# Masked float32r comparisons for the last eight source tiles in the second layer of a four-layer graph network

## The chip, the cores and the metric

The kernel runs on one core of a Trainium2 chip. The metric is the device time of one execution in microseconds (us); the kernel before takes 3552.45 us (median of three runs). The core's engines work side by side, each through its own queue in order: TensorE (PE; its weight loads are shown as PEld), VectorE (DVE), ScalarE (ACT), GpSimd (POOL), and SyncE (SP), which here only issues DMAs.

## The reference

A graph of 3327 nodes with 512 features and a 0/1 adjacency matrix goes through four layers; each adds its result to x. The first three are graph attention layers with 8, 4 and 8 heads, the fourth is a mean over neighbours with dense projections. The change lies in the second (it is called layer 1 in the code, which counts from 0):

```python
def _L1_gnn_ref(H, A, W, a_l, a_r):
    n = H.shape[0]
    mask = A + jnp.eye(n, dtype=A.dtype) > 0
    Wh = (H @ W).reshape(n, N_HEADS, D_K)             # 4 heads of 128
    sl = jnp.einsum('nhd,hd->nh', Wh, a_l)
    sr = jnp.einsum('nhd,hd->nh', Wh, a_r)
    e = jax.nn.leaky_relu(sl[:, :, None] + sr.T[None, :, :], negative_slope=0.2)
    e = jnp.where(mask[:, None, :], e, -jnp.inf)
    alpha = jnp.nan_to_num(jax.nn.softmax(e, axis=2), nan=0.0)
    out = jnp.einsum('nhm,mhd->nhd', alpha, Wh).reshape(n, 512)
    return jax.nn.elu(out)
# each layer:
h = jnp.maximum(_layernorm(x, axis=-1), 0.0)
x = x + _L1_gnn_ref(h, adj, L1_gnn_W, L1_gnn_a_l, L1_gnn_a_r)
```

## The kernel before

**The idea.** The exponential of leaky_relu(s1 + s2) is a product of a factor of the destination and a factor of the source, with one pair of factors where s1 + s2 > 0 and another where it is not. So the softmax numerator and denominator are two plain matrix products per head: a 0/2 matrix "adjacent and s1 > -s2" times the source rows with the first factor (sign a = 0), and "adjacent and s1 <= -s2" times the rows with the second (a = 1). No exponential is taken per edge; what has to be made per head are the two 0/2 matrices, transposed, with sources on the partitions.

**Tiling.** The 3327 nodes are 26 tiles of 128. Destinations are worked on in seven chunks of four tiles (`PER`; the last has two). Sources are in five groups `JG`: 6, 6, 6, 4 and 4 tiles. For each chunk c and head h (28 pairs in this layer) `attention` loads the chunk's scores s1 onto all partitions (`s1b`, line 682, two buffers), and for each sign and group the source rows (`ab`, line 714, seven buffers, ten loads per pair).

**The matrices before.** `matrices` makes, per group, a tile `tht` in fp8 (ten buffers) with one comparison per source tile and 512 destinations, on ScalarE (line 670) or, for the source tiles listed in `GP_ON_DVE`, on VectorE (line 667). In this layer the list has tiles 18 to 25, the two groups of four. A bitwise AND with the group's mask on VectorE (line 674) leaves the matrix of the first sign. The masks, fp8 zeros and twos, lie in `m` tiles (six buffers, line 271), reloaded for each chunk. When all matmuls of the first sign have read a tile, a bitwise XOR with the mask (line 794) turns it into the second sign's in place.

**The products.** `KIND = "bssvv"` says how each group is multiplied. Group 0 ("b") uses the fp8 tile as it is, against source rows in three bf16 pieces, 387 columns (line 762). The other four use float32r, 258 columns (line 759), and their matrices must be copied from fp8 to float32r: `real` does so per sign and per pass, groups 1 and 2 ("s") on ScalarE into `ts` (three buffers, 6 tiles x 256 destinations), groups 3 and 4 ("v") on VectorE into `tv` (two buffers, 4 tiles x 256 destinations), both at line 639.

A pass is two destination tiles (`ks`) against all 26 sources: per sign two passes, so four per pair, each 12 matmuls of 387 columns and 40 of 258. After a pass VectorE sums the three (or two) pieces of each accumulator into `R` (line 780). After the fourth it scales, adds and divides (lines 802 to 809). Accumulators have four buffers.

**Work in between.** After each pass `hooks.run` moves the tiles of the last finished chunk on by a stage: residual and elu (lines 866 to 870), layer norm (345 to 357), transposes (138, 142), projection for the next layer (413) and its factors (433 to 469 and 387 to 397). The order of instructions on each engine is not written out: a scheduler places them, with a few ordering hints (`after`), so an edit here can move others.

Of the kernel before, what the change touches and what calls it, by code (L numbers as in the profile page):

```python
# [29 lines left out]
FP8 = mybir.dt.float8e4  # L30
F32R = mybir.dt.float32r
AF = mybir.ActivationFunctionType
ALU = mybir.AluOpType
# [4 lines left out]
P = 128  # L38
# [4 lines left out]
S2_MAX = 30.0  # L43
S_CLIP = 40.0

GP_ON_DVE = [(5, 12, 19), tuple(range(18, 26)), (4, 9, 14, 19, 24)]


KIND = "bssvv"


@with_exitstack
def tile_gnn(ctx: ExitStack, tc: tile.TileContext, x, adj, W0, a01, W1, al, ar, W2, a2,
             Ws, bs, Wn, bn, Wc, bc, out):
    nc = tc.nc
# [8 lines left out]
    PER = 4  # L64
    chunks = [(t, min(PER, NT - t)) for t in range(0, NT, PER)]
    where = {t0 + k: (c, k) for c, (t0, n) in enumerate(chunks) for k in range(n)}
    JG = [(0, 6), (6, 6), (12, 6), (18, 4), (22, 4)]
    JM = max(n for _, n in JG)
# [45 lines left out]
    for l in range(3):  # L114
        H, DA, AO, HW = dims(l)
# [515 lines left out]
            while self.tiles or self.flying:  # L631
                self.run(1, 0, 0)

    def real(a, g, ks, th):

        nj = JG[g][1]
        k0, k1 = ks[0], ks[-1] + 1
        t = mp.tile([P, 2, nj, P], F32R, name="ts" if KIND[g] == "s" else "tv", bufs=3 if KIND[g] == "s" else 2)
        (nc.scalar.copy if KIND[g] == "s" else nc.vector.tensor_copy)(t[:, :k1 - k0, :nj], th[a][g][:, k0:k1])  # L639
        return t  # L640

    ahead = {}
# [42 lines left out]
    def attention(L, hooks, open_next, close):  # L685

        l = L.l
        H, DA, AO, HW = dims(l)
        DK = DA - 1
        masks = mask_tiles(0, l == 1) if l else masks0  # L690
        for c, (t0, nt) in enumerate(chunks):
            last = c + 1 == len(chunks)
            A = [mp.tile([P, D], F32, name="A", bufs=A_BUFS[l]) for _ in range(nt)]
            hook = 0
            for h in range(H):
# [8 lines left out]
                s1v = early.pop("s1") if "s1" in early else score_rows(l, t0, nt, h)  # L704
                ab = []
                for a in range(2 if l == 1 else 1):
                    row = []
                    for g, (_, nj) in enumerate(JG):
                        if l == 1:
                            tl = mp.tile([P, JM * 2 * DA], F32R, name="ab", bufs=7)  # L710
                            two = KIND[g] != "b"
                            w = 2 * DA if two else AO
                            v = (tl if two else tl.bitcast(BF16))[:, :nj * w].rearrange("p (j w) -> p j w", j=nj)
                            ld = nc.sync.dma_start(v.bitcast(F32) if two else v, abd[l][g][h, a])
                        else:
                            if g in ahead:
                                v = ahead.pop(g)
                            else:
                                v = pieces_tile(L, mp if l else bp, g)
                                ld = nc.sync.dma_start(v, abd[l][g][h])  # L720
                        row.append(v)
                    ab.append(row)
# [3 lines left out]
                th, flip = [[], []], []  # L726
                for g in range(len(JG)):
                    if g in early:
                        pv, gv = early.pop(g)
                    else:  # L730

                        pt = mp.tile([P, PER * JM * P], FP8, name="tht", bufs=10 if l == 1 else 7)
                        gt = pt if l == 1 else mp.tile([P, PER * JM * P], FP8, name="gt", bufs=7)
                        pv, gv, words, steps = matrices(L, nt, h, g, s1v, masks[g], pt, gt)
                        for step in steps:
                            step()
                        if l == 1:
                            flip.append(words)
                    th[0].append(pv)
                    th[1].append(gv)  # L740
                R = mp.tile([P, PER, 2, DA], F32, name="R", bufs=1)
                deg = l == 0 and h == 0
                for a in range(2 if l == 1 else 1):
                    passes = [(range(k0, min(nt, k0 + 2)), range(NT)) for k0 in range(0, nt, 2)]
                    if c == 0 and h == 0 and a == 0:
                        cut = JG[-1][0]
                        passes = [(ks, range(0, cut)) for ks, _ in passes] + [(ks, range(cut, NT)) for ks, _ in passes]
                    acc = {}
                    for ks, js in passes:
                        thr = {}  # L750
                        for j in js:
                            g, jj = jwhere[j]
                            if l == 1 and KIND[g] != "b" and g not in thr:
                                thr[g] = real(a, g, ks, th)
                            for k in ks:
                                if j == 0:
                                    acc[k] = accs.tile([P, 512], F32, name="acc")
                                if g in thr:
                                    mm = nc.tensor.matmul(acc[k][:, :2 * DA], thr[g][:, k - ks[0], jj, :], ab[a][g][:, jj, :],  # L759
                                                     start=(j == 0), stop=(j == NT - 1), skip_group_check=True)  # L760
                                elif l == 1:
                                    mm = nc.tensor.matmul(acc[k][:, :3 * DA], th[a][g][:, k, jj, :], ab[a][g][:, jj, :3 * DA],  # L762
                                                     start=(j == 0), stop=(j == NT - 1), skip_group_check=True)
                                else:
                                    o = 1 if deg else 0
                                    nc.tensor.matmul(acc[k][:, :3 * DA + o], th[0][g][:, k, jj, :],  # L766
                                                     ab[0][g][:, jj, :3 * DA + o], start=(j == 0), stop=False,
                                                     skip_group_check=True)
                                    mm = nc.tensor.matmul(acc[k][:, AO:AO + 3 * DA + o], th[1][g][:, k, jj, :],  # L769
                                                     ab[0][g][:, jj, AO:AO + 3 * DA + o], start=False, stop=(j == NT - 1),  # L770
                                                     skip_group_check=True)
                            if j == JG[3][0]:
                                late = mm.ins.name
                        if l == 2 and last and h == H - 1:
                            load_y2(yp, 0, late)
                        if js[-1] != NT - 1:
                            continue
                        for k in ks:
                            if l == 1:
                                nc.vector.tensor_reduce(R[:, k, a, :], acc[k][:, :3 * DA].rearrange("p (s d) -> p d s", s=3),  # L780
                                                        AX.X, ALU.add)
                            else:
                                v = acc[k][:, :2 * AO].rearrange("p (a w) -> p a w", a=2)[:, :, :3 * DA]
                                nc.vector.tensor_reduce(R[:, k], v.rearrange("p a (s d) -> p a d s", s=3), AX.X, ALU.add)  # L784
                            if deg:
                                n = pn(t0 + k)
                                nc.vector.tensor_reduce(deg2[:n, t0 + k:t0 + k + 1],
                                                        acc[k][:n, 3 * DA:AO + 3 * DA + 1:AO], AX.X, ALU.add)
                        gone.append(mm.ins.name)
                        hooks.run(1 if last else 3, hook, 2 if hook % 2 and c == 0 or hook % 3 == 0 and c else 1, 2 if last else 1)  # L790
                        hook += 1
                    if a == 0:
                        for pu, mu in flip:
                            nc.vector.tensor_tensor(pu, pu, mu, ALU.bitwise_xor)
                        if h == H - 1 and not last:
                            pending = loops
# [21 lines left out]
            masks = nmasks  # L818
# [79 lines left out]
    with tc.tile_pool(name="first", bufs=1) as fp:  # L898
# [19 lines left out]
        L = open_layer(0)  # L918
# [10 lines left out]
        while hooks.tiles or hooks.flying:  # L929
# [4 lines left out]
            for g in range(3):  # L934
                if n == (8, 15, 21)[g]:
# [6 lines left out]
                    s = PER * JM * P  # L942
                    pv, gv, _, steps = matrices(L, PER, 0, g, early["s1"], masks0[g], b[:, :s], b[:, s:2 * s])
                    hooks.small += steps
                    early[g] = pv, gv
        while hooks.small:
            hooks.small.pop(0)()
    A, R = [("A", D, F32, n) for n in A_BUFS], ("R", PER * 2 * 129, F32, 1)
    ab, gt, tht = ("ab", JM * 400, BF16, 7), ("gt", PER * JM * P, FP8, 7), ("tht", PER * JM * P, FP8, 7)
    tags = [[A[0], ("R", PER * 2 * 65, F32, 1), tht, ("tr", JM * P, BF16, 5), ("abx", 4 * 400, BF16, 4), gt],  # L950
            [A[1], ("ab", JM * 258, F32R, 7), R, ("ts", 2 * JM * P, F32R, 3), ("tv", 2 * 4 * P, F32R, 2), tht[:3] + (10,)],
            [A[2], ab, ("R", PER * 2 * 65, F32, 1), tht, gt]]
    hooks.masks = in_steps([mask_steps(ip, t, g) for t, g in order[20:]])
    for l in range(3):
# [3 lines left out]
        mp = att.enter_context(tc.tile_pool(name=f"att{l}", bufs=1, reuse_waits="tile"))  # L958
# [526 lines left out]
```

## Time and profile before

| what | value |
|---|---|
| runs | 3546.64, 3552.45 and 3554.89 us |
| span of the profiled execution, first to last instruction | 3551.1 us |
| granted TensorE clock, mean of the span | 0.990 |
| TensorE busy, whole span | 3442.3 us (97%) |
| VectorE busy | 2624.3 us (74%) |
| ScalarE busy | 2507.0 us (71%) |
| GpSimd busy | 618.8 us (17%) |
| first and last matmul on `ts` (line 759) | 1248.3 and 2070.1 us |
| VectorE waiting for TensorE ahead of line 639, second layer | 55.1 us in 27 waits, longest 5.5 |
| ScalarE waiting for TensorE ahead of line 639 | 52.5 us in 39 waits, longest 3.9 |
| VectorE waiting for ScalarE ahead of line 794 | 19.4 us in 13 waits, longest 4.5 |

A profile line of an instruction group reads: line of the code, engine, operation, output<-input with shapes and types, count | busy us, mean ns of one | idle time of the engine just before them, and what ended most of it. "128x1024" is 128 partitions by 1024 elements. A line of the timeline begins with the start and the length of a merged run of equal instructions, in us; in brackets stands the idle time before it and what ended it. A line of waits reads: who waited, for whom, us in total, times, longest. Matmuls overlap: one of 283 ns starts every 120 ns, so only their start times tell the rate.

### The profile page before, as it was taken

The numbers are of one execution on the slowest core, as the hardware profiler recorded it, in microseconds if no ns is written. First come the engines' busy times: TensorE is split into PE (matmuls) and PEld (weight loads), VectorE is DVE, ScalarE is ACT, GpSimd is POOL, SyncE is SP. The second block draws the span as 40 slices with busy tenths as digits, with TensorE's granted clock in tenths as the row PEclk, the third lists the DMA queues.
The fourth block names the chain that finished last, engine by engine and source line by source line (L and its number), as shares of the span: only waits on it lengthen the run. The fifth ranks groups of instructions, "written<-read, shape, count | busy, mean of one in ns | idle before, by whom it ended". The sixth has DMA issues, their size and how long they took to land. (4 is left out here: it accounts for less than half of the span.)

```text
span 3551.1 us, 77646 instructions
## 1 busy us (share of the span) xinstructions
PE 3442.3 (97%) x30751; PEld 3107.2 (88%) x30751; DVE 2624.3 (74%) x5227; ACT 2507.0 (71%) x4113; POOL 618.8 (17%) x858
## 2 busy tenths in 40 slices
PE   7899999999999999999999989999999999999998
PEld 6789999999999888888888869989898989876887
DVE  7788888888887699888888868867676768672121
ACT  5777787878787789888888677767666757572111
POOL 6611222112111202222223320101010101020000
PEclk9999999999999999999999999999999999999999
DMA  7699999999857787777777875555545555576331
GB/s 207 223 282 251 233 263 238 268 260 250 256 203 247 246 285 276 279 269 273 269 273 254 332 268 190 191 175 189 183 166 181 185 172 188 168 271 257 105 107 54
DMA packets 398120, 797.72 MB, mean 225 GB/s; under 512 B 112970, under 2 KB 221845, under 8 KB 397105
## 3 DMA queue, kind: packets, MB, share of 16 engines
q1 hardware_dynamic: 363890, 723.14, 63.4%
q0 software_dynamic: 28128, 62.42, 7.6%
q10 hardware_dynamic: 5726, 7.08, 0.6%
q8 instruction: 245, 4.01, 0.5%
q14 instruction: 131, 1.07, 0.1%
HBM read 663.59 MB, written 129.64 MB: 223 GB/s over the span
## 5 line engine op out<-in xcount | busy, mean ns | idle before, releaser
L670 ACT ACTIVATE gt<-s1b,ks 128x512 fp8e4<-128x512 f32 (+1 forms) x2448 | 1448.2, 677 | 276.4 <-issue 160.1
L766 PE MATMUL acc<-ab,tht 128*128 128x195 bf16 (+1 forms) x9112 | 1553.1, 248 | 5.4 <-DVE tht L674 4.6
L769 PE MATMUL acc<-ab,gt 128*128 128x195 bf16 (+1 forms) x9112 | 1552.2, 248 | 5.0 <-DVE rc L806 3.3
L769 PEld LDWEIGHTS <-gt 128*128 128x128 fp8e4 x10744 | 1053.6, 98 | 40.1 <-issue 27.4
L766 PEld LDWEIGHTS <-tht 128*128 128x128 fp8e4 x10744 | 1053.4, 98 | 24.8 <-DVE tht L674 11.5
L674 DVE TENSOR_TENSOR tht<-gt,m 128x768 uint32<-128x768 uint32 (+3 forms) x557 | 445.5, 800 | 129.4 <-ACT gt L670 125.5
L676 DVE TENSOR_TENSOR gt<-tht,m 128x768 uint32<-128x768 uint32 (+3 forms) x557 | 448.0, 805 | 8.7
L639 ACT CAST ts<-tht 128x1536 fp32r<-128x1536 fp8e4 x208 | 300.0, 1470 | 55.6 <-PE acc L759 52.5
L759 PE MATMUL acc<-ab,ts 128*128 128x258 f32 x2496 | 333.4, 289 | 4.7 <-ACT ts L639 3.4
L759 PEld LDWEIGHTS acc<-ab,ts 128*128 128x128 f32 x2496 | 313.2, 190 | 13.2 <-ACT ts L639 3.8
L667 DVE TENSOR_SCALAR gt<-s1b,ns 128x512 fp8e4<-128x512 f32 (+1 forms) x446 | 218.2, 495 | 129.4 <-PE acc L769 125.1
L1021 PE MATMUL acc<-y,mf 128*128 128x512 f32 x1352 | 309.8, 391 | 1.1 <-DVE mf L1016 1.1
L670 ACT ACTIVATE tht<-s1b,ks 128x512 fp8e4<-128x512 f32 (+1 forms) x504 | 308.4, 680 | 2.3 <-DMA s1b<-s 1.7
L1021 PEld LDWEIGHTS acc<-y,mf 128*128 128x128 f32 x1352 | 253.6, 188 | 57.2 <-DVE mf L1016 1.5
L769 PE MATMUL acc<-abx,gt 128*128 128x195 bf16 (+1 forms) x1632 | 287.4, 249 | 11.6 <-DVE rc L806 5.6
L766 PE MATMUL acc<-abx,tht 128*128 128x195 bf16 (+1 forms) x1632 | 287.8, 249 | 4.6 <-DVE tht L674 3.0
L869 POOL TENSOR_TENSOR xt<-xt,e 128x512 f32<-128x512 f32 x72 | 121.9, 1693 | 916.8 <-DVE e L868 583.9
L784 DVE TENSOR_REDUCE R<-acc 128x130 f32<-128x390 f32 x416 | 214.2, 554 | 79.5 <-PE acc L769 78.9
L762 PE MATMUL acc<-ab,tht 128*128 128x387 bf16 x1248 | 225.8, 329 | 8.9 <-DMA ab<-ab 5.8
L1018 ACT CAST mf<-m 128x768 fp32r<-128x768 fp8e4 (+1 forms) x78 | 59.1, 762 | 244.5 <-PE acc L1021 232.7
L759 PE MATMUL acc<-ab,tv 128*128 128x258 f32 x1664 | 218.8, 283 | 1.4 <-DVE tv L639 1.2
L759 PEld LDWEIGHTS acc<-ab,tv 128*128 128x128 f32 x1664 | 207.2, 189 | 2.9 <-DVE tv L639 2.1
(163 smaller groups left out, 3710.2 us busy)
## 6 DMA issues: line engine op xcount, KB each, us to landing
ab<-ab SPq DMA_DIRECT2D x333, 600.0 KB, 5.3
ab<-ab SPq DMA_DIRECT2D x112, 774.0 KB, 6.5
ab<-ab SPq DMA_DIRECT2D x112, 516.0 KB, 5.3
ab<-ab SPq DMA_DIRECT2D x112, 400.0 KB, 4.0
abx<-ab SPq DMA_DIRECT2D x110, 400.0 KB, 7.9
ab<-ab SPq DMA_DIRECT2D x56, 582.0 KB, 7.3
s1b<-s SPq DMA_DIRECT2D x120, 256.0 KB, 6.5
m<-mask SPq DMA_DIRECT2D x69, 384.0 KB, 4.4
```

What stands on the lines that cost most here:

```text
L639: (nc.scalar.copy if KIND[g] == "s" else nc.vector.tensor_copy)(t[:, :k1 - k0, :nj], th[a][g][:, k0:k1])
L667: nc.vector.tensor_scalar(gv[:, :, jj, :], s1v, L.ns2[:, j, h:h + 1], 2.0, op0=ALU.is_gt, op1=ALU.mult, saturate=False)
L670: nc.scalar.activation(gv[:, :, jj, :], s1v, AF.Relu, bias=L.ks2[:, j, h:h + 1], scale=BIG, saturate=False)
L674: nc.vector.tensor_tensor(pu, gu, mu, ALU.bitwise_and)
L676: nc.vector.tensor_tensor(gu, pu, mu, ALU.bitwise_xor)
L759: mm = nc.tensor.matmul(acc[k][:, :2 * DA], thr[g][:, k - ks[0], jj, :], ab[a][g][:, jj, :], start=(j == 0), stop=(j == NT - 1), skip_grou ...
L762: mm = nc.tensor.matmul(acc[k][:, :3 * DA], th[a][g][:, k, jj, :], ab[a][g][:, jj, :3 * DA], start=(j == 0), stop=(j == NT - 1), skip_grou ...
L766: nc.tensor.matmul(acc[k][:, :3 * DA + o], th[0][g][:, k, jj, :], ab[0][g][:, jj, :3 * DA + o], start=(j == 0), stop=False, skip_group_che ...
L769: mm = nc.tensor.matmul(acc[k][:, AO:AO + 3 * DA + o], th[1][g][:, k, jj, :], ab[0][g][:, jj, AO:AO + 3 * DA + o], start=False, stop=(j == ...
L784: nc.vector.tensor_reduce(R[:, k], v.rearrange("p a (s d) -> p a d s", s=3), AX.X, ALU.add)
L869: nc.gpsimd.tensor_add(xt, xt, e)
L1021: nc.tensor.matmul(acc[k], mf[:, jj, :], y2[g][:, jj, s, :], start=(j0 + jj == 0 and s == 0), stop=(j0 + jj == NT - 1 and s == 1))
```

## The change

For groups 3 and 4, now of kind "d", no fp8 matrix is made any more: no comparison of 512 destinations, no AND, no XOR, no copy. Instead `real` makes the float32r tile of one pass and one sign directly, with one VectorE instruction per source tile of 2 x 128 destinations: it compares s1 with the source's -s2 (greater for the first sign, less or equal for the second) and multiplies the result by the mask. The tile is called `td`, has two buffers and the size of `tv`. `GP_ON_DVE` is empty for this layer. The space of two `tht` buffers goes to an eighth `ab` buffer. The matmuls, their operands' types and their values stay.

```diff
-GP_ON_DVE = [(5, 12, 19), tuple(range(18, 26)), (4, 9, 14, 19, 24)]
+GP_ON_DVE = [(5, 12, 19), (), (4, 9, 14, 19, 24)]
-KIND = "bssvv"
+KIND = "bssdd"
+TD = 2
...
-    def real(a, g, ks, th):
-
-        nj = JG[g][1]
+    def real(L, a, g, ks, th, h, s1v, mask):
+
+        j0, nj = JG[g]
         k0, k1 = ks[0], ks[-1] + 1
-        t = mp.tile([P, 2, nj, P], F32R, name="ts" if KIND[g] == "s" else "tv", bufs=3 if KIND[g] == "s" else 2)
-        (nc.scalar.copy if KIND[g] == "s" else nc.vector.tensor_copy)(t[:, :k1 - k0, :nj], th[a][g][:, k0:k1])
+        if KIND[g] == "d":
+            t = mp.tile([P, 2, nj, P], F32R, name="td", bufs=TD)
+            for jj in range(nj):
+                nc.vector.scalar_tensor_tensor(t[:, :k1 - k0, jj, :], s1v[:, k0:k1, :], L.ns2[:, j0 + jj, h:h + 1],
+                                               mask[:, k0:k1, jj, :], op0=ALU.is_le if a else ALU.is_gt, op1=ALU.mult)
+            return t
+        t = mp.tile([P, 2, nj, P], F32R, name="ts", bufs=3)
+        nc.scalar.copy(t[:, :k1 - k0, :nj], th[a][g][:, k0:k1])
         return t
...
-                            tl = mp.tile([P, JM * 2 * DA], F32R, name="ab", bufs=7)
+                            tl = mp.tile([P, JM * 2 * DA], F32R, name="ab", bufs=8)
...
+                    elif l == 1 and KIND[g] == "d":
+                        pv = gv = None
                     else:
 
-                        pt = mp.tile([P, PER * JM * P], FP8, name="tht", bufs=10 if l == 1 else 7)
+                        pt = mp.tile([P, PER * JM * P], FP8, name="tht", bufs=8 if l == 1 else 7)
...
-                                thr[g] = real(a, g, ks, th)
+                                thr[g] = real(L, a, g, ks, th, h, s1v, masks[g])
```

The list of pool sizes at line 951 follows: `ab` 8, `td` in place of `tv`, `tht` 8.

More of the change, by code (lines that the diff above doesn't have):

```diff
@@ L950, in tile_gnn @@
     tags = [[A[0], ("R", PER * 2 * 65, F32, 1), tht, ("tr", JM * P, BF16, 5), ("abx", 4 * 400, BF16, 4), gt],
-            [A[1], ("ab", JM * 258, F32R, 7), R, ("ts", 2 * JM * P, F32R, 3), ("tv", 2 * 4 * P, F32R, 2), tht[:3] + (10,)],
+            [A[1], ("ab", JM * 258, F32R, 8), R, ("ts", 2 * JM * P, F32R, 3), ("td", 2 * 4 * P, F32R, TD), tht[:3] + (8,)],
             [A[2], ab, ("R", PER * 2 * 65, F32, 1), tht, gt]]
```

## The prediction

> **What bounds the kernel now.** I read the page first (engine shares), then the busy time by stretches to find the second layer and its limit, then the TensorE timeline inside it, the VectorE groups of its undisturbed part, and last the waits. The second layer runs from about 1233 to 2072 us. Stretches out of it (length, then busy us and count of PE, PEld, DVE, ACT, POOL, then clock, DMA share, GB/s):
>
> ```profile
> 1233.00:1360.00 127.00, 124.98 (x893) 106.36 (x894) 116.46 (x227) 115.50 (x147) 4.13 (x10) 0.99 0.80 284
> 1480.00:1600.00 120.00, 119.81 (x876) 105.56 (x876) 105.31 (x195) 103.62 (x135) 33.22 (x37) 1.00 0.78 276
> 1960.00:2072.00 112.00, 100.86 (x686) 86.63 (x686) 85.45 (x184) 74.70 (x127) 35.90 (x47) 0.97 0.90 332
> ```
>
> TensorE is busy for all but 0.2 of 120 us in the middle and loses 11 us only at the layer's end; VectorE and ScalarE stand at 88% and 86%. A busy share can hide slow matmuls, so I looked at the timeline:
>
> ```profile
> 1602.42 3.19 PE L759 MATMUL acc<-ab,ts 128*128 128x258 f32 x24
> 1605.44 2.08 PE L759 MATMUL acc<-ab,tv 128*128 128x258 f32 x16
> 1607.36 2.15 PE L762 MATMUL acc<-ab,tht 128*128 128x387 bf16 x12
> 1609.21 3.18 PE L759 MATMUL acc<-ab,ts 128*128 128x258 f32 x24
> 1612.22 2.07 PE L759 MATMUL acc<-ab,tv 128*128 128x258 f32 x16
> ```
>
> One pass (two destination tiles against all 26 sources) takes 1609.21 - 1602.42 = 6.79 us and follows the last without a gap. So this layer is bound by TensorE, whose matmuls the change leaves as they are in number and shape: 104 passes of 6.79 us are 706 us, and 26 tiles projected for the next layer at 4.0 us (16 matmuls of 0.22 us, 4 transposes of 0.11) are 104. Of the layer's 839 us, 839 - 810 = 29 us at most are not such matmuls, and part of those is the weight fusion of line 190 (7 us). That caps what the change can bring.
>
> **The cost of the change.** VectorE's groups of the middle 600 us (1360 to 1960 us), 19 pairs of chunk and head (152 copies, 8 per pair):
>
> ```profile
> L639 DVE CAST tv<-tht 128x1024 fp32r<-128x1024 fp8e4 x152 | 107.5, 708 | 41.3 <-PE acc L759 41.3
> L667 DVE TENSOR_SCALAR tht<-s1b,ns 128x512 fp8e4<-128x512 f32 x148 | 74.8, 553 | 0.9 <-PE acc L762 0.9
> L794 DVE TENSOR_TENSOR tht<-tht,m 128x768 uint32<-128x768 uint32 x59 | 57.1, 968 | 13.4 <-ACT ts L639 13.2
> L674 DVE TENSOR_TENSOR tht<-tht,m 128x512 uint32<-128x512 uint32 x38 | 28.0, 739 | 0.6 <-DMA m<-mask 0.2
> L794 DVE TENSOR_TENSOR tht<-tht,m 128x512 uint32<-128x512 uint32 x38 | 24.6, 680 | 0.0
> L450 DVE TENSOR_TENSOR AB<-mm,AB 128x512 f32<-128x512 f32 x38 | 24.3, 680 | 0.0
> ```
>
> *Removed:* the copies, the comparisons and the 512-wide ANDs and XORs, 107.5 + 74.8 + 28.0 + 24.6 = 234.9 us, or 12.4 us per pair.
>
> *Added:* per pair 2 signs x 2 passes x 2 groups x 4 tiles = 32 masked comparisons of 128x256 elements (896 for 28 pairs, less 64 because the last chunk has one pass: 832). The trace has no such instruction. Its nearest rows are two-input operations of the same width, and, for the per-partition scalar that it reads, line 1030, which has one, against line 493, which has none; both read 512 elements from PSUM:
>
> ```profile
> L674 DVE TENSOR_TENSOR tht<-gt,m 128x256 uint32<-128x256 uint32 x32 | 13.5, 421 | 6.5 <-ACT gt L670 6.3
> L1030 DVE SCALAR_TENSOR_TENSOR o<-acc,rdeg,y 128x512 f32<-128x512 f32 x25 | 18.8, 751 | 67.9 <-PE acc L1021 67.8
> L493 DVE TENSOR_TENSOR AB<-mm,bias 128x512 f32<-128x512 f32 x26 | 17.9, 687 | 42.2 <-PE mm L486 28.1 <-DMA y<-AB 14.1
> ```
>
> 421 + (751 - 687) = 485 ns alone. Instructions in a row overlap: the 38 of line 450 stand in twos and take 24.3 us, not 38 x 0.680 = 25.8, so each pair saves 0.08 us. In a run one therefore costs 0.40 us, and 32 cost 12.8 us when all stand in runs, 15.5 when all stand alone; 0.34 us (no charge for the scalar) and 10.9 us is the lower end. In the built programs most stand in runs of two to eight, so I take 13.4 us: 1.0 us more per pair than is removed, between -1.5 and +3.1. The rows removed contain their delays by GpSimd (553 against a median of 479 ns for the comparison), mine do not; that makes it about +2.
>
> The page "VectorE: DVE Perf Modes" of the Trainium skill (section on the TRN2 errata) gives 58 cycles plus one per element at 0.96 GHz, an estimate of 327 ns each and 10.5 us per pair. By it VectorE would gain 2 us per pair; the rows above, with a scalar at 64 ns and a fixed part of 421 - 256/0.96 = 154 ns, speak for the dearer price.
>
> *What hides it.* In these 600 us VectorE idles 600 - 527 = 73 us, 3.8 per pair, of which 41.3 (2.2 per pair) is its copy waiting for TensorE to free a buffer: it ran ahead. That is the cover; +2 us per pair uses nearly all of it, and +3.1 is more than it by 0.9 us, or 24 us over 26 pairs' worth of work.
>
> *How it is spread.* The order of the built programs shows it. I cut VectorE's queue after each pass's last float32r tile and priced the pieces by start-to-start times (0.60 copy, 0.40 to 0.43 comparison, 0.87 and 0.60 AND/XOR, 0.94 two reductions of line 780, 2.7 for lines 802 to 809, 3.8 for a projected tile). A steady chunk, 16 passes, before: 9.8 4.8 6.0 5.6 6.7 6.3 7.2 5.2 3.6 8.3 10.4 5.4 2.8 11.6 6.4 4.7, sum 105 us; after: 9.9 5.3 6.9 7.1 8.9 4.7 7.4 4.7 9.5 5.8 8.5 6.2 9.2 7.2 7.0 4.9, sum 113. TensorE takes 16 x 6.79 + 4 x 4.0 = 125. So 84% becomes 90%, more evenly spread. But seven passes (9.5 to 7.0) hold 53.4 us against 7 x 6.79 + 2 x 4.0 = 55.5 of TensorE, 96%, before any wait. The last chunk's eight passes hold 68 us (62 before) against 8 x 6.79 + 4 x 4.0 = 70.
>
> *What moves.* Comparison, AND and XOR were done a pair ahead and could slip; now all 3.2 us per pass come after TensorE has freed the one of two "td" buffers, 5.8 us (6.79 less that group's 0.96) before it is wanted again. Behind them on VectorE's queue stand the AND and XOR of the other three groups, for which ScalarE's float32r copies wait, and the reductions that free the accumulators. The XOR itself waits for ScalarE (13.2 us in the 600, 0.7 per pair), and that wait now delays comparisons behind it.
>
> ```profile
> 1766.44 1.23 PE L759 MATMUL acc<-ab,tv 128*128 128x258 f32 x8 [0.51 <-DVE tv L639]
> 1785.11 1.23 PE L759 MATMUL acc<-ab,tv 128*128 128x258 f32 x8 [0.71 <-DVE tv L639]
> ```
>
> These two are nearly all the stalls that TensorE now has from VectorE in the 600 us: 1.2 us. Each is about 0.6 us. I take 0.4 us per pair in the steady part (two stalls in three pairs): 24 x 0.4 = 10 us, and 3 us in the last chunk, from 0 to 24 + 8 over both.
>
> *Small edits.* The eighth "ab" buffer lets a load start one group earlier. The wait to gain from, of the weight loads in this layer (us in total, times, longest), of which I count -3 (0 to -6):
>
> ```profile
> PEld L762 <- DMA ab<-ab: 6.5, 3, 3.2
> ```
>
>  Eight "tht" buffers for three tiles per pair are 2.7 pairs where ten for five were 2: nothing, since VectorE and ScalarE were never seen waiting for one. The row of scores (two buffers) and the masks of the last two groups are now read until a pair's last pass, so their reloads (line 682, line 271) issue later; on SP's queue the "ab" loads stand behind them. The reload of a mask takes 3.4 us and is wanted 5 us later: nothing, up to +5 at six chunk changes if a load behind it is late. ScalarE, GpSimd and TensorE issue the same instructions as before.
>
> *Sum:* +10 + 3 - 3 = +10 us. The profiled span is 3551.1 us and the runs' median 3552.45, so 1.4 us lie around it: **3562 us**, 0.3% slower.
>
> **Rivals.** (1) *The cover holds* (no change): TensorE remains gapless because the new spread is flatter (highest piece 9.9 for 11.6) and 90% is under 100%. For it: gapless TensorE at 88%; against: the 96% stretch and the waits for ScalarE. +1 us for a few stalls less -3 of loads plus 3 at the end: 3553. (2) *Faster:* the masked comparison costs 0.34 us, so VectorE is 1.5 us per pair lighter, and the layer's end, where TensorE loses 11 of 112 us to chains through VectorE and ScalarE, shortens by half (-5), with loads -4: 3543. It decides from a price below about 0.37 us (11.8 in runs). Against it: the 64 ns of the scalar. (3) *VectorE becomes the bound:* alone-standing instructions and GpSimd's delays bring the price to 0.48, +3.1 us or more per pair; less the cover +24, with 8 at the end: 3584. (4) The rewrite not doing what it says is out: 832 masked comparisons stand in the built program, the copies and their comparisons not.
>
> **Numbers.** Forecast 0.45 (3555 to 3575), rival 1 0.27, rival 2 0.13, rival 3 0.15. A measurement of this kernel tells 0.2%, 7 us, from no change. Faster is rival 2 without its small cases, 0.12; slower is rival 3 and four fifths of the forecast and a little of rival 1, 0.54; same is the rest, 0.34. The range takes in rival 1, and rivals 2 and 3 but for their outer parts: 3545 to 3590.
>
> **What would show it.** The masked comparison's row: 480 ns alone, 400 between starts. VectorE near 90% or above in the layer, its waits for TensorE's buffers well below 41 us in 600. TensorE's idle time "until DVE td" of some 10 us in pieces below 1 us. Wrong if the row shows 420 ns (then rival 1 or 2), if TensorE's gaps end on ScalarE's copies or on loads, or if times move outside 1233 to 2072 us.

## The result, and the profile after

The changed kernel takes 3578.55 us (median of 4 runs, 3568.18 to 3584.44) against 3553.48 us (4 runs of the kernel before, with the three shown above among them): a ratio of 1.007 with a 95% interval of 1.0051 to 1.009. It is slower by 25 us; the forecast was 10. The profiled execution has a span of 3566.4 us and is the quickest of the four. Its first layer is 8 us shorter than in the profile of before. That layer's program is the same in both, and over the profiles of this study it takes 1223 to 1241 us whatever the kernel, so nothing is read from it. The second layer, from its first to its last matmul, goes from 838.8 to 859.4 us.

Busy time by stretches of the changed kernel, in the same columns as before; the first and the last stretch are moved with the layer's own start and end:

```profile
1225.00:1352.00 127.00, 123.68 (x862) 103.60 (x863) 109.90 (x246) 101.04 (x128) 6.25 (x10) 0.99 0.77 266
1480.00:1600.00 120.00, 118.96 (x857) 103.38 (x856) 113.22 (x238) 107.06 (x144) 30.45 (x37) 1.00 0.76 270
1972.00:2084.00 112.00, 96.84 (x635) 81.92 (x633) 92.57 (x196) 72.63 (x122) 34.49 (x45) 0.94 0.85 308
```

VectorE (third busy number) rises from 105.3 to 113.2 of 120 us in the middle, 94%. TensorE's busy time (first) hardly shows the loss there, 119.0 for 119.8, since a matmul that comes a little late still overlaps the next; its count does, 857 matmuls in place of 876. At the layer's end it loses 15 of 112 us where it lost 11.

VectorE's largest groups of the middle 600 us, 1360 to 1960 us:

```profile
L642 DVE SCALAR_TENSOR_TENSOR td<-s1b,ns,m 128x256 fp32r<-128x256 f32 x602 | 286.3, 525 | 32.9 <-PE acc L768 32.9
L789 DVE TENSOR_REDUCE R<-acc 128x129 f32<-128x387 f32 x150 | 76.2, 548 | 0.0
L681 DVE TENSOR_TENSOR tht<-tht,m 128x768 uint32<-128x768 uint32 x57 | 53.0, 948 | 0.3 <-ACT tht L677 0.2
L803 DVE TENSOR_TENSOR tht<-tht,m 128x768 uint32<-128x768 uint32 x57 | 52.3, 948 | 0.0
```

The 602 masked comparisons (18.8 pairs at 32) replace the copies, the comparisons and the 512-wide ANDs and XORs. They take 286.3 us of VectorE, 0.476 us each and 15.2 per pair, where 12.4 were removed. The median length over the layer is 476 ns; the mean of 525 holds delays by GpSimd, up to 1.5 us.

What TensorE's weight loads waited for, over the whole layer. First the kernel before (its lines 759 and 762), then the changed one (768 and 771); a row says what the idle time ended on, in us, how often, and the longest:

```profile
PEld L762 <- DMA ab<-ab: 6.5, 3, 3.2
PEld acc L759 <- ACT ts L639: 3.8, 1, 3.8
PEld L762 <- DVE tht L674: 3.1, 2, 2.2
PEld acc L759 <- DVE tv L639: 2.1, 4, 0.9
```

```profile
PEld acc L768 <- ACT ts L646: 18.4, 13, 5.6
PEld acc L768 <- DVE td L642: 11.2, 37, 0.9
PEld L771 <- DVE tht L681: 7.0, 3, 3.6
```

The matmul behind a late weight load shows the same stall once more in a row of its own, somewhat shorter (on the casts 3.4 us once before and 13.2 us in 12 waits after), so the rows of PE and PEld must not be added.

Waits for VectorE's own matrices went from 2.1 to 11.2 us, which is the forecast's mechanism. Waits for the matrices that ScalarE casts went from 3.8 to 18.4 us, and those for the fp8 matrices that VectorE's AND and XOR finish, from 3.7 to 7.7 us (a few smaller rows included). The 6.5 us of waiting for source rows are gone. These four changes add up to 21.2 us, near the 20.6 by which the layer grew. ScalarE's cast over the layer, before and after, the last part being what the cast itself waited for:

```profile
L639 ACT CAST ts<-tht 128x1536 fp32r<-128x1536 fp8e4 x208 | 300.0, 1470 | 55.6 <-PE acc L759 52.5 <-DVE rc L806 1.4 <-DVE tht L794 0.9
```

```profile
L646 ACT CAST ts<-tht 128x1536 fp32r<-128x1536 fp8e4 x208 | 297.8, 1469 | 69.9 <-DVE tht L681 27.4 <-PE acc L768 18.0 <-DVE tht L803 14.7
```

208 casts of 1.47 us in both. Before, they ran ahead and waited 52.5 us for TensorE to free a buffer, and 0.9 us for VectorE's XOR. After, they wait 42.1 us for VectorE's AND (line 681) and XOR (line 803), and only 18.0 for TensorE. The casts have lost their head start. Not each of these waits reaches TensorE: the three longest, 7.1, 5.7 and 5.7 us at 1478, 1606 and 1734 us, are not followed by a gap of TensorE on a cast.

Where in the layer the time is lost is read by putting the starts of the same line's matmuls side by side (the first, second, third float32r matmul and so on, of one kernel against the other). The differences to the kernel before grow by 4.3 us from 1248 to 1368 us (the change from the first chunk of destinations to the second), by 9.1 us from 1368 to 1982 us (the steady part) and by 7.0 us from there to the last one at 2072 us (into the short last chunk): 20.4 us. In the steady part the waits of the weight loads account for it, 14.1 us against 4.6 before: 7.6 for "td" in 30 waits (2.1 for "tv" before), and 6.5 for casts (none before), in two waits of 0.6 and 1.0 us at each of four changes of chunk. Lines of the timeline at the first and the last place, in the changed kernel:

```profile
1309.49 0.72 ACT L677 ACTIVATE tht<-s1b,ks 128x512 fp8e4<-128x512 f32 x1 [10.31 <-DMA s1b<-s]
...
1330.42 3.14 PE L768 MATMUL acc<-ab,ts 128*128 128x258 f32 x24 [2.18 <-ACT ts L646]
...
2010.33 3.10 PE L771 MATMUL acc<-ab,tht 128*128 128x387 bf16 x12 [3.38 <-DVE tht L681]
...
2018.32 4.57 PE L768 MATMUL acc<-ab,ts 128*128 128x258 f32 x24 [4.89 <-ACT ts L646]
```

ScalarE stood 10.3 us for a load of the scores, which SP issued at 1305 us behind ten loads of "ab". Over the layer its comparisons waited 19.0 us for scores; before, 1.7.

At the layer's end the long gaps cost more than their own length. The 12 matmuls behind the gap of 3.38 us took 3.10 us and the 24 behind the one of 4.89 took 4.57, where they take 2.15 and 3.18 in the steady lines of before. The clock granted to TensorE is 0.53 from 2011 to 2022 us. Over the last stretch it is 0.93 (0.96 before), which makes some 7 of 97 us (4 of 90 before), part of them inside the gaps. In the steady part it is 1.00 in both kernels.

### The profile page after: what moved, and what is told of

Its sections match the earlier page's. It is cut to its first block, busy times and chain, and to the rows that moved or that the text cites. A ratio compares the mean times of both kernels' runs of the same rounds, so it can differ in the third digit from the quotient of the medians.

```text
span 3566.4 us, 77996 instructions
## 1 busy us (share of the span) xinstructions
PE 3454.2 (97%) x30751; PEld 3108.6 (87%) x30751; DVE 2681.5 (75%) x5515; ACT 2503.7 (70%) x4113; POOL 602.8 (17%) x858
## 5 line engine op out<-in xcount | busy, mean ns | idle before, releaser
L642 DVE SCALAR_TENSOR_TENSOR td<-s1b,ns,m 128x256 fp32r<-128x256 f32 x832 | 390.9, 520 | 46.5 <-PE acc L768 46.5
L768 PE MATMUL acc<-ab,ts 128*128 128x258 f32 x2496 | 333.6, 290 | 13.2 <-ACT ts L646 13.2
L768 PEld LDWEIGHTS acc<-ab,ts 128*128 128x128 f32 x2496 | 313.8, 191 | 24.7 <-ACT ts L646 18.4
L878 POOL TENSOR_TENSOR xt<-xt,e 128x512 f32<-128x512 f32 x72 | 108.6, 1508 | 866.0 <-DVE e L877 620.1
L768 PE MATMUL acc<-ab,td 128*128 128x258 f32 x1664 | 231.1, 287 | 3.4 <-DVE td L642 2.8
```

The source lines that it names most:

```text
L642: nc.vector.scalar_tensor_tensor(t[:, :k1 - k0, jj, :], s1v[:, k0:k1, :], L.ns2[:, j0 + jj, h:h + 1], mask[:, k0:k1, jj, :], op0=ALU.is_le ...
```

## Experiments

Three theories were open. Theory 1: the price of VectorE's work, GpSimd's delays included. Theory 2: late scores at the change of a chunk. Theory 3: the order of the work, with masked comparisons standing ahead of ANDs and XORs that ScalarE's casts need. The table has all runs; the last three columns are the drift against the kernel before in the three stretches named above, from one profile each.

| run | median us | ratio to before, 95% interval | first change | steady | end |
|---|---|---|---|---|---|
| the change | 3578.55 | 1.0070 (1.0051 to 1.0090) | +4.3 | +9.1 | +7.0 |
| e1_rings_back | 3581.93 | 1.0082 (1.0062 to 1.0102) | +8.1 | +7.4 | +14.6 |
| e2_rings_only | 3562.05 | 1.0021 (1.0008 to 1.0034) | -1.8 | +8.0 | +6.5 |
| e3_no_scalar | 3601.20 | 1.0130 (1.0109 to 1.0151) | +1.2 | +32.8 | +12.3 |
| e4_td3 | 3575.72 | 1.0066 (1.0045 to 1.0087) | +5.5 | +7.0 | +14.0 |
| e5_no_scalar_pinned | 3592.60 | 1.0104 (1.0074 to 1.0133) | +2.9 | +23.6 | +5.2 |
| e6_td3_pinned | 3571.25 | 1.0046 (1.0032 to 1.0061) | +5.1 | +5.7 | +4.6 |
| e7b_small_add | 3565.46 | 1.0028 (1.0016 to 1.0040) | +6.0 | +2.1 | +5.6 |
| e8_wide | 3586.85 | 1.0091 (1.0061 to 1.0122) | +2.7 | +22.5 | +7.0 |
| e11_before_small_add | 3544.69 | 0.9973 (0.9961 to 0.9985) | +0.5 | -2.0 | -0.9 |
| e12_no_scalar_small_add | 3577.87 | 1.0063 (1.0046 to 1.0080) | +4.9 | +20.2 | +3.3 |
| e13_free_scores | 3585.22 | 1.0089 (1.0072 to 1.0106) | +6.1 | +16.2 | +7.6 |
| e14_wide3 | 3584.82 | 1.0084 (1.0066 to 1.0102) | +5.1 | +19.2 | +4.7 |

**The rings.** e1 is the changed kernel with the old numbers of buffers, e2 the kernel before with the new ones.

```diff
-tl = mp.tile([P, JM * 2 * DA], F32R, name="ab", bufs=8)
-pt = mp.tile([P, PER * JM * P], FP8, name="tht", bufs=8 if l == 1 else 7)
+tl = mp.tile([P, JM * 2 * DA], F32R, name="ab", bufs=7)
+pt = mp.tile([P, PER * JM * P], FP8, name="tht", bufs=10 if l == 1 else 7)
```

> The masked comparisons as in the changed kernel, but the rings as before: seven ab buffers and ten tht. Theory (VectorE is too full and its comparisons come just in time): the same loss as the changed kernel, 3570 to 3585 us, TensorE waiting some 10 to 15 us for td and 25 to 35 us for ts in the layer. Rival (the smaller tht ring or the moved loads cause the loss): back to 3553 to 3560 us.

> The kernel before with the new rings alone: eight ab buffers, eight tht (1.6 pairs of five tiles instead of 2). Theory (VectorE): within 5 us of before, 3549 to 3558. Rival (rings): slower by 10 us or more, since the same rings would then cost the same there.

e1 lies 3 us above the changed kernel, with overlapping intervals and nearly the same order of instructions (24 of VectorE's 1652 in the layer stand elsewhere): the old rings don't bring the loss back down, so the new ones don't cause it. e2 missed its expectation of 3549 to 3558: the kernel before gets slower by 0.2%, 10 us between the medians, which is where its rival began. Its second layer takes 849.9 us in place of 838.8. There five matrices of a pair still pass through "tht", so eight of them are fewer than two pairs; in the changed kernel three do. But the scheduler has also moved 258 of VectorE's 1372 instructions of the layer, and VectorE's work is the same as before. Whether the ring or the order costs these 11 us isn't shown. So a moved order can't be ruled out as a part of the 20.6 us that the change costs.

**Price and buffer, with the order free.** e3 compares with a constant, e4 has a third "td" buffer in place of the eighth "ab".

```diff
-nc.vector.scalar_tensor_tensor(t[:, :k1 - k0, jj, :], s1v[:, k0:k1, :], L.ns2[:, j0 + jj, h:h + 1],
+nc.vector.scalar_tensor_tensor(t[:, :k1 - k0, jj, :], s1v[:, k0:k1, :], 0.0,
...
-TD = 2
+TD = 3
```

> The changed kernel with the comparison against the constant 0 instead of the source's own score (this leaves out the source's score in the last eight tiles, so the result is another; all else is the same work). Theory (VectorE's load): one masked comparison falls from 476 to about 415 ns, 832 of them take 50 us off VectorE's queue in the layer, its share falls from 94% to about 88%, and the time returns to 3553 to 3562 us. Rival (the score row and the masks are held until a pair's last pass, and their late reload starves ScalarE): nothing is released earlier, 3570 to 3585.

> The changed kernel with three td buffers instead of two, paid for with the eighth ab buffer. If VectorE has time enough and only the narrow window of two buffers makes it late: TensorE's waits for td fall below 3 us, the time to 3553 to 3565. If its total load is the limit (94% busy): the waits change little, 3570 to 3582. Late score rows as the cause: 3570 to 3585 with the waits for ts unchanged.

The row fell to 416 ns in e3, and the kernel became 23 us slower. In e4 TensorE's weight loads no longer waited for "td", but still 17.4 us for ScalarE's casts, and their waits for ANDs and XORs at line 771 rose from 7.7 to 20.5 us, one of them 10.2; no time was gained. In both the scheduler had put more than 160 of VectorE's instructions alone in other places, so neither tells price from order. In the runs marked pinned, and in e7b, e11 and e12, the second layer's instructions were therefore held in the order of the kernel compared with, on every engine (a ScalarE copy and some GpSimd instructions apart). No run holds the order without another edit.

**The same two edits in the changed kernel's order.**

> The changed kernel with one edit: the masked comparison compares with the constant 0.0 instead of with the per-partition scalar (so the matrices of the last eight source tiles are made from the sign of the scores and are wrong; nothing else is left out). Unlike in the earlier run of this edit, the instructions of the second layer are held in exactly the changed kernel's order on every engine, so only the duration of one kind of instruction differs. Estimate of its row: about 415 ns instead of 476 on the median. Theory 1 (the price: VectorE is so full that 60 ns on each of 32 instructions of a pair, 1.9 us per pair or 46 us of VectorE in 24 pairs, set most of the loss): second layer 859 us in the changed kernel goes to 840 to 848, and the time to 3553 to 3565; TensorE's 16.8 us of gaps that end on td fall below 8. Theory 2 (late scores and masks at the change of a chunk, which hold ScalarE's comparisons back): the gaps at the chunk changes near 1300 to 1355 us and 2005 to 2020 us stay, the time is 3570 to 3580. Theory 3 (the order itself: the masked comparisons stand in VectorE's queue ahead of ANDs and XORs that ScalarE's casts need): about the changed kernel's time, at least 3572, with the same gaps on ts.

> The changed kernel with a third buffer for td and, for its room, six buffers instead of eight for tht, the second layer's instructions in the changed kernel's order on every engine (one copy on ScalarE apart). Theory 1 (the price of VectorE's work): a third buffer makes no work shorter; the time stays within 6 us of the changed kernel, 3572 to 3584, although the gaps on td become fewer. Theory 3 (the masked comparisons wait for TensorE to give a td buffer back and so hold up the ANDs and XORs behind them): VectorE's idle time ahead of the masked comparison, 46.5 us in 600, falls below 20, TensorE's gaps on ts and td (31.8 and 16.8 us) fall by half, the time is 3550 to 3562. If six buffers of tht are too few, the gaps on tht grow instead (5.5 us in the changed kernel) and the run tells nothing of the third buffer.

e5 falls outside all three expectations: a shorter instruction in the same queues, and 14 us more. The timeline of e5 at the end of a chunk:

```profile
1495.98 2.09 DVE L642 SCALAR_TENSOR_TENSOR td<-s1b,m 128x256 fp32r<-128x256 f32 x6
1496.14 5.66 POOL L878 TENSOR_TENSOR xt<-xt,e 128x512 f32<-128x512 f32 x1 [1.43 <-DVE e L877]
1497.99 2.68 DVE L803 TENSOR_TENSOR tht<-tht,m 128x768 uint32<-128x768 uint32 x3
...
1501.83 0.63 ACT L875 ACTIVATE e<-A 128x512 f32<-128x512 f32 x1 [7.57 <-POOL xt L878]
...
1506.99 4.65 PE L768 MATMUL acc<-ab,ts 128*128 128x258 f32 x24 [4.29 <-ACT ts L646]
```

GpSimd's addition to the rows of x, 1.45 us on the median, took 5.66. ScalarE's next exponential needs the buffer "e" that the addition reads, stood 7.57 us for it, and its casts stood behind that; TensorE lost 4.29 us. Behind the gap the granted clock was 0.62 from 1507.0 to 1511.5 us, and 24 matmuls took 4.65 us in place of 3.19. This repeats at four chunk ends (additions of 5.66 us four times, gaps of 4.29 to 4.30 us four times). The same place in the changed kernel:

```profile
1489.37 3.48 DVE L642 SCALAR_TENSOR_TENSOR td<-s1b,ns,m 128x256 fp32r<-128x256 f32 x6
1489.53 1.45 POOL L878 TENSOR_TENSOR xt<-xt,e 128x512 f32<-128x512 f32 x1 [1.61 <-DVE e L877]
...
1491.02 0.63 ACT L875 ACTIVATE e<-A 128x512 f32<-128x512 f32 x1 [3.54 <-POOL xt L878]
```

Here the six comparisons took 3.48 us (six undisturbed ones take 2.46, at 1305.8 us), and the addition its 1.45. In both runs the comparisons began 0.16 us before the addition. With the per-partition scalar VectorE gives way to GpSimd; with the constant it does not. Why is not shown. e3 has the same stalls (four additions of 5.99 us).

For "td" the shorter instruction does what theory 1 says: in the steady part the weight loads' waits for it fall from 7.6 to 1.8 us. But their waits for casts rise from 6.5 to 18.7 us, and the granted clock falls from 1.00 to 0.98 of these 638 us, an estimate of 10 to 16 us. Together these explain the extra 14.5 us of drift in the steady part.

In e6 the third buffer (its room comes from "tht", and the waits at line 771 don't grow, 7.4 us) takes away every wait of the masked comparison in the middle stretch (VectorE's row there):

```profile
L642 DVE SCALAR_TENSOR_TENSOR td<-s1b,ns,m 128x256 fp32r<-128x256 f32 x608 | 294.6, 534 | 0.0
```

The weight loads still wait 8.0 us for "td" over the layer (11.2 before that) and 17.5 us for ScalarE's casts (18.4). The median is 7 us below the changed kernel, with overlapping intervals, and the second layer 5 us shorter. VectorE waits 30.7 us for TensorE at its reductions instead. So the buffer is a small part, the wait for it isn't what makes the casts late, and theory 3 in its strong form (3550 to 3562) falls.

**GpSimd's addition cut to 8 columns,** in the changed kernel (e7b), in the kernel before (e11), and in the changed kernel with the constant (e12).

```diff
-nc.gpsimd.tensor_add(xt, xt, e)
+(nc.gpsimd.tensor_add(xt[:, :8], xt[:, :8], e[:, :8]) if l == 1 else nc.gpsimd.tensor_add(xt, xt, e))
```

> The changed kernel with GpSimd's addition to the rows of x in the second layer cut to 8 columns (so those rows keep the rest of the layer before: left out is most of the second layer's residual sum), in the changed kernel's order. Theory of GpSimd delays (part of theory 1): masked comparisons that run beside this addition take 1.0 to 1.5 us more; their mean of 525 ns in the second layer's steady stretch falls towards the 476 ns of an undisturbed one, 1 us or more per pair, and the time falls by 5 to 15 us, to 3562 to 3573. Without it: the mean falls by less than 10 ns or the time stays within 4 us of the changed kernel's 3576 to 3582.

> The control of the run with GpSimd's short addition: the kernel before, in its own order, with GpSimd's addition to the rows of x in the second layer cut to 8 columns (left out is most of that layer's residual sum). If the collision of VectorE with this addition is a cost that the change made, the kernel before loses little by it and gains little here: 0 to 4 us, 3549 to 3555, and the second layer stays within 3 us of 838.8. If every kernel pays it (the kernel before shows additions of up to 4.6 us, mean 2.15), the gain is as large as in the changed kernel, 9 to 15 us, 3539 to 3546, and then the collision explains none of the 25 us of difference.

> Both edits in the changed kernel's order: the masked comparison against the constant 0.0 (wrong matrices of the last eight tiles) and GpSimd's addition in the second layer cut to 8 columns (left out is most of that layer's residual sum). The run with the constant alone was slower, 870.6 us in the second layer, because the additions were starved for 5.66 us each time a chunk ended and ScalarE stood behind them. If that is right, these stalls are gone here: no gap of TensorE over 3 us between 1400 and 1980 us, and the true worth of 60 ns less per masked comparison shows against the run with the short addition alone (852.8 us): theory 1 (price) says 843 to 849 and 3553 to 3561; if the price of the instruction decides nothing once the collision is away, 851 to 855 and 3562 to 3569. If the stalls of 4.3 us stay, the starving of the addition wasn't their cause.

The changed kernel gains 13 us by it, as expected, and the mean of its masked comparisons falls from 525 to 502 ns. But the control gains 9. Its time fits the case in which every kernel pays (3539 to 3546), its second layer the one in which the change pays (within 3 us of 838.8). In both, part of this lies behind the second layer: from its last matmul to that of the third layer it takes 3.8 us less in e7b and 6.1 us less in e11. The third layer works on other values then; whether that is the reason isn't shown. In the second layer itself e7b gains 6.6 us (859.4 to 852.8) and e11 2.4 (838.8 to 836.4). So the collision with this addition explains about 4 of the 20.6 us that the change costs there. In the steady part the drift falls from 9.1 to 2.1 us, with -2.0 in the control: 4.1 of the 9.1 us are left. TensorE's waits for casts there fall from 6.5 to 1.7 us (none in the control, with or without the edit), those for "td" only from 7.6 to 6.7. So in the steady part the casts are late mostly by way of this addition, which the exponential ahead of them waits for, and what is left is mainly "td".

e12 missed its expectation: the stalls stayed, at 3.2 us. Its timeline:

```profile
1501.15 2.09 DVE L642 SCALAR_TENSOR_TENSOR td<-s1b,m 128x256 fp32r<-128x256 f32 x6
1501.32 4.59 POOL L878 TENSOR_TENSOR xt<-xt,e 128x8 f32<-128x8 f32 x1 [1.43 <-DVE e L877]
1503.16 2.68 DVE L803 TENSOR_TENSOR tht<-tht,m 128x768 uint32<-128x768 uint32 x3
...
1505.94 0.63 ACT L875 ACTIVATE e<-A 128x512 f32<-128x512 f32 x1 [6.50 <-POOL xt L878]
```

An addition of 8 columns, 0.2 us elsewhere in the same run, takes 4.59 us: it ends at 1505.91, when VectorE's last two-input instruction (1503.16 + 2.68 = 1505.84) does. It isn't the addition's length that is paid but the wait for the end of VectorE's row of two-input instructions. This is the main cost of the constant in e5 and e12; e3 has the same long additions, in an order of its own. In the control, which has no masked comparisons, an addition of 8 columns at 1368.45 us beside three XORs and an AND took 2.60 us and ended 0.06 us after the AND: such rows shut GpSimd out there too.

**Late scores.** In e13 the second pass of a pair reads a constant row in place of the scores.

```diff
-s1v[:, k0:k1, :]
+(bias[:, :2 * P].rearrange("p (k i) -> p k i", k=2)[:, :k1 - k0] if k0 else s1v[:, k0:k1, :])
```

> The changed kernel with the masked comparisons of the second pass of a pair reading a constant row in place of the scores (half of the matrices of the last eight tiles are wrong), so that the scores' buffer comes free after the first pass; the order is the scheduler's own, and differs in some places. Theory 2 (late scores at the change of a chunk): ScalarE's waits for the load of the scores, 19.0 us (longest 10.3) in the changed kernel, fall below 5; the gaps near 1310 to 1368 and 1982 to 2072 us, worth 6.4 and 7.0 us against the kernel before, fall to 2 or less each; the time goes to 3563 to 3570. Without it (the load stands where it does because of the queue ahead of it and not because of the masked comparisons): the waits stay above 10 us and the time within 5 us of the changed kernel, or it moves for reasons of order.

ScalarE's waits for the scores rose, to 53.8 us in 17 waits:

```profile
  ACT tht L677: 53.8, 17
```

The buffer was free earlier, yet the load stood no better: SP issued the second chunk's first load at 1309.5 us, again behind ten loads of "ab". So giving up the masked comparison's hold on the scores doesn't make them earlier. Their place in SP's queue is the likelier reason, but it isn't shown: in e13 the order differs too (445 of VectorE's 1652 instructions), and an earlier place wasn't tried.

**Fewer, wider masked comparisons.** e8 makes the matrices of both passes at once; e14 gives them a third buffer.

```diff
-t = mp.tile([P, 2, nj, P], F32R, name="td", bufs=TD)
+t = both[a, g] = mp.tile([P, PER, nj, P], F32R, name="td", bufs=TD)
-nc.vector.scalar_tensor_tensor(t[:, :k1 - k0, jj, :], s1v[:, k0:k1, :], L.ns2[:, j0 + jj, h:h + 1],
+nc.vector.scalar_tensor_tensor(t[:, :nt, jj, :], s1v, L.ns2[:, j0 + jj, h:h + 1],
```

> The changed kernel with the masked comparison over both passes' targets at once: 16 instructions of 128x512 for a pair instead of 32 of 128x256 (the tile td is twice as large, two buffers; for its room ab and tht have seven buffers). Estimate from the rows of 128x256: if a third of the 476 ns doesn't depend on the width, one takes about 0.8 us, 12.7 us per pair instead of 15.2. Theory 1 (price): VectorE's share falls from 94% to about 91% of the steady stretch and the time goes to 3555 to 3568. Theory 3 (order and buffers): td is now made once for two passes, so its wait for TensorE comes once in place of twice, but a buffer stays taken for two passes and the masked comparisons of the next sign or pair wait longer; 3570 to 3600.

> The masked comparison over both passes at once (128x512) with three buffers for td; for their room six buffers each for ab and tht. With two buffers VectorE had less to do (803 ns for 512 columns, 85% busy in the steady stretch) but TensorE lost 34 us in gaps on td and the second layer took 869.5 us. If the buffers were the cause, the gaps on td fall below 10 us, the second layer takes 838 to 850, and the time 3550 to 3565: the change would then be about even with the kernel before. If six buffers of ab are too few, gaps that end on loads of ab take their place and the time stays above 3575.

```profile
L644 DVE SCALAR_TENSOR_TENSOR td<-s1b,ns,m 128x512 fp32r<-128x512 f32 x295 | 226.6, 803 | 48.0 <-PE acc L772 44.9 <-issue 2.9
```

The price falls as estimated, to 12.3 us per pair (15.2 with the narrow ones), and VectorE is busy 85% of the middle 600 us, less than in the kernel before (88%). Both versions are slower than the change all the same. TensorE's weight loads wait 25.3 us for "td" in e8. In e14 they wait 6.5 us for it, as was expected, but 8.2 for loads of "ab" (six buffers) and 9.3 at line 772 with no cause shown, and the second layer takes 868.0 us. Their order is the scheduler's own, so they don't tell width from order. No version tried beats the kernel before, other than by leaving out work.

## Why the prediction was right and where it fell short

- *Direction and range.* Slower by more than 0.2%, and 3578.55 us lies within 3545 to 3590. The forecast's own 3555 to 3575 was missed by 4 us, and rival 3 (3584) came out nearer than the forecast (3562).
- *The price* was near: 13.4 us per pair and one more for GpSimd's delays, for a measured 15.2. One instruction alone took 476 ns (485 estimated), seven in an undisturbed row 2.82 us (0.40 each, as taken), and the scalar costs what the two rows at 512 elements said (60 ns for 64). VectorE's busy time per pair went from 527.3/19 = 27.75 to 564.2/18.8 = 30.0 us, +2.25 for "about +2".
- *The page* "VectorE: DVE Perf Modes" of the Trainium skill gave an estimate of 327 ns by its section on the TRN2 errata; the same section says that this row under-predicts the duration of a single operation. The trace decides against the row here: 416 ns with a constant, 476 with a per-partition scalar.
- *TensorE's stalls on "td"* were forecast as 10 us in pieces below 1 us in the steady part. Right in kind, too large in size: the weight loads' waits there went from 2.1 to 7.6 us, and over the layer from 2.1 to 11.2 in 37 pieces, the longest 0.9.
- *The steady part as a whole* was forecast at +10 and drifted by +9.1, but that agreement is partly luck. Only 5.5 us of TensorE's added waiting there is for "td", and 6.5 is for casts. With a third buffer in the same order 5.7 us of drift are left, and with the short addition 4.1 against its control.
- *The other road to TensorE* is the step that failed. The text named the ANDs and XORs that stand behind the masked comparisons, and ScalarE's casts behind those, and then priced only "td". Over the layer this road is the larger one: +14.6 us of TensorE's waits for casts and +4.0 for the fp8 matrices, against +9.1 for "td". In the steady part it runs mostly through GpSimd's addition and the exponential behind it, which the prediction left out. "Wrong if TensorE's gaps end on ScalarE's copies" came true for that part.
- *The cover* of 2.2 us per pair, VectorE's copy waiting for TensorE, was to be nearly used up. It wasn't: "well below 41 us in 600" was forecast for this wait and 32.9 found, 1.75 per pair. Nor was it what made the casts late, since e6 takes it away and TensorE's waits for casts stay. That the engine ahead sometimes waits doesn't say that its work comes in time.
- *The ends.* Nothing, "up to +5 at six chunk changes", and +3 in the last chunk were too little: +4.3 at the first change and +7.0 at the end. Scores did come late (19.0 us of ScalarE's waiting), but e13 gives no sign that the hold named in the forecast was the reason. The lowered clock behind long gaps is in none of the prediction's terms.
- *The eighth "ab" buffer,* -3 us: the 6.5 us of waiting for source rows did go, but in e1, with seven buffers, they are gone as well, so it wasn't the buffer. "Never seen waiting" for a "tht" buffer overlooks 0.9 us in the prediction's own row of line 667; nothing came of it.
- *Rival 3* is nearest by its time, and its price of 0.48 us is the measured one; its mechanism isn't the one shown. If VectorE's throughput were the bound, the wide comparisons (2.9 us less work per pair) should have been quicker. They were slower, though in an order of their own.

What stays open: how much of the 4.3 and 7.0 us at the two ends is the order that the scheduler chose, how much the late loads and how much the clock; and what the order alone is worth in the layer as a whole, which e2 leaves possible as a part.

## What to carry to other kernels

An engine at 90% that feeds two others in one queue is judged by what stands behind each new wait, not by its share: price the road through every engine that it feeds. A change of one instruction's length moves a scheduler's whole order, so an experiment on a price needs the order held, and a control of the same edit in the kernel before: here the control took away two thirds of an effect that looked like the cause (13 us against 9). A stall of TensorE stands in two rows, that of the weight load and that of the matmul: add up one of them only, and see whether the sum fits the time lost.

## What the runs showed of the hardware

- A masked comparison of 128x256 takes 476 ns with a per-partition scalar and 416 ns with a constant; one of 128x512 with the scalar takes 744 ns on the median.
- With the constant, a row of two-input VectorE instructions shut GpSimd's two-input addition out from end to end, 4.59 us for 8 columns; with the per-partition scalar GpSimd got through in its usual 1.45 us and VectorE paid, 3.48 us for six instead of 2.46. The page "SBUF — State Buffer" of the Trainium skill (section "Who interferes with whom") says that a VectorE instruction with two SBUF inputs contends with a GpSimd instruction that reads SBUF, and that the loser blocks for the whole instruction. The trace agrees that they block each other, and adds that a row without gaps acts like one long instruction.
- The clock granted to TensorE fell to about half for some us behind gaps: 0.62 over 4.5 us behind one of 4.29 (e5), 0.53 over the 11 us around the gaps of 3.38 and 4.89 at the changed kernel's end. No threshold follows from these runs: behind a gap of 2.18 us it was 1.00 over 5 us in the changed kernel and 0.66 in e7b.
- Taking 60 ns off a frequent instruction made the kernel 14 us slower in the same order of instructions: by longer waits on casts at four changes of chunk and the lower clock behind them.
